# Moving a rarely taken branch, gathering every second tile in parts, and turning the biases later in a one-core attention and mixture-of-experts kernel

## The chip, the cores and the metric

The kernel runs on one core of a Trainium2 chip. The metric is the device time of one execution in microseconds (us). The time before is 1584.31 us, the median of 4 runs (1583.06 to 1585.34). A profile of one further execution was taken. Its engines are PE (TensorE matmul; PEld is its weight load), DVE (VectorE), ACT (ScalarE), POOL (GpSimd) and SP (SyncE, which issues DMAs).

## The reference, cut to what matters

The input is one image of 256 channels and 48 x 48 pixels, so 2304 tokens of width 256. All is float32.

```
x = x + Attn0(group_norm(x))            # 4 heads; softmax over all 9216 head-rows
t = tokens(x)                           # (2304, 256)
t = t + Attn1(layer_norm(t))            # soft slices: 64 slices, 8 heads
t = t + MoE(layer_norm(t))
out = t transposed back to (1, 256, 48, 48)

MoE(xf):                                # E = 8 experts, top 2 of each token
    top_w, top_i = top_k(xf @ Wg + bg, 2);  top_w = softmax(top_w)
    for e in range(8):
        h   = gelu(xf @ W1[e] + b1[e])              # 256 -> 1024
        out = out + w_dense[:, e] * (h @ W2[e] + b2[e])   # 1024 -> 256
```

## The kernel before, in words

**Start (lines 248 to 345).** The group norm needs a mean and a variance per group of 8 channels. DVE collects `bn_stats` as the image lands; PE multiplies the channel means and then `dm` (variance plus squared difference of means) with the group matrix `gm`, into the small PSUM tile `pgb`; DVE adds epsilon (`ve`, line 228), POOL raises it to the power -0.5 (`rstd`, line 229), and DVE norms the image block by block (`xn`, line 311). PE then projects q and k (lines 320 and 324) into a ring of five PSUM tiles `pp`. While PE would have nothing to do, `busy_first(n)` (line 265) gives it n matmuls whose results are not used: 14 at the very start, and 2 between the two group matmuls (line 297). They are written into the same tile `pgb` as the group sums. The 78 rows of biases (`brow`) are turned to columns (`bcol`) by a PE transposition in `spread()` (line 293), also into `pgb`. Helper classes (`InOrder`, line 52, whose issue line is L60) keep the order of `pe`, `dve`, `act` and `pool` calls as written; calls through `nc.*` are placed by a scheduler.

**Middle.** Attention 0 and the slice attention follow, and the routing: each token is given two slots, sorted by expert, in tiles of 128 slots. `slot_t` tells the token row of each slot of each tile; `used` is how many tiles are in use. Before the experts start, `busy(8, spin)` (line 1202) again gives PE eight matmuls of no use.

**Experts (lines 1343 to 1419).** There are at most 43 tiles. 36 are always there (`SURE` = 36: tiles 0 to 35), tiles 36 to 38 are "near" (`FAR` = 39), and tiles 39 to 42 are rare. For each tile s:

- `rows` gathers 128 token rows of 1 KB with one indirect DMA from POOL; `parts` instead does it with four indirect DMAs of 256 B per row (line 1237 issues all of these), so that DVE can turn the tile (`turn_parts`, line 1287) in place of PE (`turn`, line 1278: two PE transpositions into `pt` and a DVE copy to `xT`). `in_parts(s)` (line 1254) says which: before, tiles 2 to 35 except 5, 9, 13, ..., 33.
- `load_w1` has SP load 1 MB of the tile's expert (ring of two); `first` does 16 matmuls `ph` and 8 Gelus on ACT (`hid`); `second` does 8 matmuls `py`, with a function `meanwhile` called after the third of them, and DVE makes `y`; `scatter` adds `y` to the token rows in memory `t_d` by an indirect DMA from POOL.

The order is: gathers of 36, 37, 38, 0 and 1; the number `used` is loaded into every engine (line 1350); four nested branches `tc.If(used > s)` skip the rare tiles (line 1355); then tile 36, the branches for 37 and 38 (line 1386), and the loop over tiles 0 to 35 (line 1395), in which `first(s)` stands ahead of `second(s - 1)`. A tile is gathered two tiles ahead of its use. In this execution 39 tiles are in use: tiles 37 and 38 are worked on and the rare ones are jumped over.

**End (lines 1421 to 1459).** The token rows are read back after the scatter of tile 34, turned by PE, and written out. A last branch (line 1479) jumps over a second, safer version of the whole program.

Of the kernel before, what the change touches and what calls it, by code (L numbers as in the profile page):

```python
# [9 lines left out]
FP = mybir.dt.float32  # L10
# [5 lines left out]
P = 128  # L16
# [49 lines left out]
def layers(  # L66
# [181 lines left out]
    with proj, tc.tile_pool(name="ps_pj", bufs=5, space=PSUM) as ps_pj, tc.tile_pool(  # L248
# [11 lines left out]
            nc.scalar.copy(dst, pw)  # L260
            return dst

        pgb = ps_g.tile([P, 512], FP, name="pgb")

        def busy_first(n):
            for _ in range(n):
                pe.matmul(
                    pgb[:, 256:512], ones, ones.unsqueeze(1).to_broadcast([P, 2, P]), start=True, stop=True
                )

        busy_first(14)
        WqT = transposed(pj.tile([P, 2, C], FP, name="WqT"), raws["Wq"])
        pg = pgb[:, 0:4].rearrange("p (a b) -> p a b", a=2)
        pb = pgb[:, 16:94]

        st = pj.tile([P, 2, 6, 6], FP, name="st")
        mv = pj.tile([P, 2, 2], FP, name="mv")
# [12 lines left out]
        mean = pj.tile([P, 2], FP, name="mean")  # L290
        dve.tensor_copy(mean, pg[:, 0, :])

        def spread():
            pe.matmul(pg[:, 1, :], gm, dm, start=True, stop=True)
            pe.transpose(pb, brow, ident[0:78, 0:78])

        busy_first(2)
        spread()
        WkT = transposed(pj.tile([P, 2, C], FP, name="WkT"), raws["Wk"])
        rstd = pj.tile([P, 2], FP, name="rstd")  # L300
        rsqrt(rstd, pg[:, 1, :], 1e-5, 2)
        xn = t_flat[:, 0 : 2 * NT].rearrange("p (c n) -> p c n", c=2)
        dve.tensor_copy(bcol, pb)
        bq8 = pj.tile([P, 2], FP, name="bq8")
        dve.tensor_scalar(bq8, bcol[:, B_Q : B_Q + 2], 0.125, None, ALU.mult)
        WvT = transposed(pj.tile([P, 2, C], FP, name="WvT"), raws["Wv"])

        for bi, (t0, tn) in enumerate(TBLOCKS):
            toks = slice(t0, t0 + tn)
            for c in range(2):  # L310
                nc.vector.tensor_scalar(
                    xn[:, c, toks], x_sb[:, c, toks], mean[:, c : c + 1], rstd[:, c : c + 1],
                    ALU.subtract, ALU.mult,
                )
            for m in range(2):
                cols = slice(m * P, (m + 1) * P)
                pq = ps_pj.tile([P, 512], FP, name="pp", tag="pp")
                pk = ps_pj.tile([P, 512], FP, name="pp", tag="pp")
                for c in range(2):
                    nc.tensor.matmul(  # L320
                        pq[:, 0:tn], WqT[:, c, cols], xn[:, c, toks], start=(c == 0), stop=(c == 1)
                    )
                for c in range(2):
                    nc.tensor.matmul(
                        pk[:, 0:tn], WkT[:, c, cols], xn[:, c, toks], start=(c == 0), stop=(c == 1)
                    )
                for j in range(2):
                    rows = slice(j * DK, (j + 1) * DK)
                    at = (2 * m + j) * NT + t0
                    for half in range(2):  # L330
                        dst = q2[half * DK : (half + 1) * DK, at : at + tn]
                        if j == 1 and half == 1:
                            nc.scalar.activation(
                                dst, pq[rows, 0:tn], AF.Identity, bias=bq8[rows, m : m + 1], scale=0.125
                            )
                        else:
                            nc.vector.tensor_scalar(  # L337
                                dst, pq[rows, 0:tn], bcol[rows, B_Q + m : B_Q + m + 1], 0.125,
                                ALU.add, ALU.mult,
                            )  # L340
                bk_m = bcol[:, B_K + m : B_K + m + 1]
                nc.scalar.activation(kk[:, m, toks], pk[:, 0:tn], AF.Identity, bias=bk_m)
            if bi == 0:
                later_constants()
                transposed(WoT, raws["Wo"])
# [73 lines left out]
    def busy(n, bank):  # L419

        for _ in range(n):
            pe.matmul(bank[:, 0:256], ident, Wqkv_sb[:, 0, 0:256], start=True, stop=True)
# [627 lines left out]
    with gating, tc.tile_pool(name="onehot", bufs=1) as oh, tc.tile_pool(  # L1050
# [148 lines left out]
                pq[:, k, :], quad[:, k, :, :].rearrange("p q s -> p (q s)"), empties, start=True, stop=True,  # L1199
            )  # L1200
        dve.tensor_scalar(part_t, pq, 4.0, quarter, ALU.mult, ALU.add)
        busy(8, spin)

    def expert_of(s, engine):
        return nc.values_load(
# [5 lines left out]
    with tc.tile_pool(name="ps_h", bufs=1, space=PSUM) as ps_h, tc.tile_pool(  # L1211
# [5 lines left out]
        def ring(pool, n, shape, name):  # L1217
            return cycle([pool.tile(shape, FP, name=f"{name}{k}") for k in range(n)])

        ring_xs, ring_w1 = ring(fp, 2, [P, C], "xs"), ring(fp, 2, [P, 2, HID], "w1")  # L1220
        ring_xT, ring_hid = ring(fp, 3, [P, 2, P], "xT"), ring(fp, 2, [P, NHC, P], "hid")
        ring_y = ring(fp, 2, [P, C], "y")
        ring_ph, ring_py = ring(ps_h, 3, [P, 4, P], "ph"), ring(ps_y, 2, [P, C], "py")
# [2 lines left out]
        near_xs = iter([fp.tile([P, C], FP, name=f"near_xs{s}") for s in range(SURE, FAR)])  # L1226
        fin = ctx.enter_context(tc.tile_pool(name="fin", bufs=1))
        far_xs, far_w1 = fin.tile([P, C], FP, name="far_xs"), fin.tile([P, 2, HID], FP, name="far_w1")
        here = fin.tile([P, NT], FP, name="here")
        held = fin.tile([P, NTT], FP, name="held")  # L1230
        obs = cycle([fin.tile([P, 2, 512], FP, name=f"ob{k}") for k in range(3)])
# [20 lines left out]
            return xs  # L1252

        def in_parts(s):
            return 2 <= s < SURE and s % 4 != 1

        def parts(s, xs):

# [16 lines left out]
            )  # L1275
            return w1

        def turn(xs):

            pt = next(ring_pt)  # L1280
            for c in range(2):
                pe.transpose(pt[:, c, :], xs.rearrange("p (d c) -> p c d", c=2)[:, c], ident)
            xT = next(ring_xT)
            dve.tensor_copy(xT, pt)
            return xT

# [7 lines left out]
                )  # L1294
            return xT

        def first(s, xT, w1):

            e = expert_of(s, mybir.EngineType.Activation)
            hid = next(ring_hid)  # L1300
            for f0 in range(0, NHC, 4):
                ph = next(ring_ph)
                for f in range(f0, f0 + 4):
                    for c in range(2):
                        pe.matmul(
                            ph[:, f - f0, :], w1[:, c, f * P : (f + 1) * P], xT[:, c, :],
                            start=(c == 0), stop=(c == 1),
                        )
                for f in range(f0, f0 + 4):
                    act.activation(  # L1310
                        hid[:, f, :], ph[:, f - f0, :], AF.Gelu, bias=b1_e[:, bass.ds(e, 1), f],
                    )
            return hid
# [32 lines left out]
            xs[s] = rows(s, next(near_xs))  # L1346
        for s in range(2):
            w1[SURE + s] = load_w1(SURE + s, next(ring_w1))
            xs[s] = parts(s, next(ring_xs))
        used = nc.values_load(  # L1350
            used_i, min_val=0, max_val=NSL,
            skip_runtime_bounds_check_because="it is a sum of counts, cut at NSL",
        )

        with ExitStack() as more:
            for s in range(FAR, NSL):
                more.enter_context(tc.If(used > s))
                issued.clear()
                far = turn(rows(s, far_xs))
                scatter(s, second(s, first(s, far, load_w1(s, far_w1)), lambda: None))  # L1360
        issued.clear()

        def turn_next(s):
            if s in xs:
                xT[s] = (turn_parts if in_parts(s) else turn)(xs.pop(s))
# [17 lines left out]
        hid[SURE] = first(SURE, xT.pop(SURE), w1.pop(SURE))  # L1383
        w1[SURE + 2] = load_w1(SURE + 2, next(ring_w1))
        scatter(SURE, second(SURE, hid.pop(SURE), more_turns))
        with ExitStack() as more:
            for s in near[1:]:
                more.enter_context(tc.If(used > s))
                issued.clear()
                hid[s] = first(s, xT.pop(s), w1.pop(s))  # L1390
                scatter(s, second(s, hid.pop(s), lambda: turn_next(s + 1) if s + 1 in near else None))
        issued.clear()
        for s in range(2):
            w1[s] = load_w1(s, next(ring_w1))
        for s in range(SURE):
            hid[s] = first(s, xT.pop(s), w1.pop(s))
            if s + 2 < SURE:
                xs[s + 2], w1[s + 2] = parts(s + 2, next(ring_xs)), load_w1(s + 2, next(ring_w1))
            if s == 0:
                turn_next(1)  # L1400
            elif s < SURE - 2:
                scatter(s - 1, second(s - 1, hid.pop(s - 1), lambda: turn_next(s + 1)))
            if SURE - 3 <= s < SURE - 1:

                scatter(s, second(s, hid.pop(s), lambda: turn_next(s + 1) if s == SURE - 2 else None))
            if s == 4 and bad is not None:
                judge()
            if s == 6:
                dve.tensor_scalar(
                    held, lim[:, 0:NTT], -1.0, empties[:, SURE - 1 : SURE], ALU.mult, ALU.add  # L1410
                )
            if 8 <= s < 8 + len(TBLOCKS):
                t0, n = TBLOCKS[s - 8]
                shape = [P, n // P, P]
                dve.tensor_tensor(
                    here[:, t0 : t0 + n].rearrange("p (k r) -> p k r", r=P),
                    steps.unsqueeze(1).to_broadcast(shape),
                    bc(held[:, t0 // P : (t0 + n) // P], shape), ALU.is_equal,
                )
# [96 lines left out]
```

## Time and profile before

| What | Value |
|---|---|
| Median of 4 runs | 1584.31 us |
| The profiled execution's own time | 1586.42 us |
| Its span, first to last instruction | 1584.7 us |
| Mean granted clock of TensorE | 0.997 |
| PE busy | 1563.3 us (99%), 13105 matmul records |
| DVE, ACT, POOL busy | 66%, 52%, 17% |
| Experts' stage, by the timeline | 1279 us to 1558 us |
| Matmuls `ph` / `py` | 147.3 us x1248 / 142.8 us x624 |
| Gathers in parts | x104 (26 tiles), 1021 ns each on POOL |

A line of the groups reads: line, engine, operation, tiles out<-in, shapes, count | busy us, mean ns of one | idle time of the engine just before, and what ended it. A line of the waits reads: engine and tile <- what it waited for: total us, times, longest. The trace has two records for one float32 matmul, each with its weight load, and one for a PE transposition. A row whose engine ends in q is the sequencer's: it dispatches to the engine, loads registers and branches, and may be ahead of the engine. The granted clock is given by stretch of time; 0.50 means that PE ran at half speed.

### The profile page before, as it was taken

The numbers are of one execution on the slowest core, as the hardware profiler recorded it, in microseconds if no ns is written. First come the engines' busy times: TensorE is split into PE (matmuls) and PEld (weight loads), VectorE is DVE, ScalarE is ACT, GpSimd is POOL, SyncE is SP. The second block draws the span as 40 slices with busy tenths as digits, with TensorE's granted clock in tenths as the row PEclk, the third lists the DMA queues.
The fourth block names the chain that finished last, engine by engine and source line by source line (L and its number), as shares of the span: only waits on it lengthen the run. The fifth ranks groups of instructions, "written<-read, shape, count | busy, mean of one in ns | idle before, by whom it ended". The sixth has DMA issues, their size and how long they took to land. (4 is left out here: it accounts for less than half of the span.)

```text
span 1584.7 us, 32306 instructions
## 1 busy us (share of the span) xinstructions
PE 1563.3 (99%) x13105; PEld 782.0 (49%) x13105; DVE 1038.3 (66%) x1323; ACT 830.0 (52%) x1168; POOL 270.0 (17%) x210
## 2 busy tenths in 40 slices
PE   9999999999999999999999999999999999999998
PEld 5633343333333333333333333333334689999996
DVE  7578787787777778878778778787787721211111
ACT  3356565555666556656556566566554433333331
POOL 0001001011010110110101101101010135767671
PEclk9999999999999999999999999999999999999999
DMA  4000000000000000000000000000000946666765
GB/s 137 1 1 1 1 1 3 7 1 1 9 1 1 8 1 2 7 2 2 4 5 2 2 8 1 1 8 1 1 2 16 333 143 193 194 183 186 192 178 162
DMA packets 53071, 79.32 MB, mean 50 GB/s; under 512 B 22719, under 2 KB 43406, under 8 KB 47790
## 3 DMA queue, kind: packets, MB, share of 16 engines
q1 hardware_dynamic: 42834, 66.45, 13.0%
q0 software_dynamic: 9424, 10.10, 3.9%
q8 instruction: 108, 1.77, 0.4%
q10 hardware_dynamic: 652, 0.56, 0.1%
q14 instruction: 53, 0.43, 0.1%
HBM read 62.94 MB, written 12.32 MB: 47 GB/s over the span
## 5 line engine op out<-in xcount | busy, mean ns | idle before, releaser
L60 ACT ACTIVATE p<-s 128x1024 f32<-128x1024 f32 x648 | 662.7, 1023 | 471.1 <-PE s L60 470.0
L60 DVE TENSOR_TENSOR acc<-acc,p 128x1024 f32<-128x1024 f32 x612 | 749.5, 1225 | 243.3 <-ACT p L60 237.3
L60 PE MATMUL av<-p,v_sb 64*64 64x512 f32 x5184 | 676.0, 590 | 3.4 <-ACT p L60 2.2
L60 PE MATMUL s<-q,kk 64*64 64x512 f32 x5184 | 675.0, 589 | 0.5 <-DVE tn L60 0.5
L60 PEld LDWEIGHTS s<-q,kk 64*64 64x64 f32 x5184 | 202.2, 133 | 353.5 <-issue 181.5
L60 PEld LDWEIGHTS av<-p,v_sb 64*64 64x64 f32 x5184 | 195.7, 131 | 358.8 <-ACT p L60 201.4
L60 POOL PARTITION_ALL_REDUCE total<-both x17 | 71.2, 4186 | 1012.0 <-ACT p L60 833.8
L60 ACT ACTIVATE hid<-ph,bcol 128x128 f32<-128x128 f32 x312 | 89.1, 368 | 197.8 <-PE ph L60 193.7
L60 PEld LDWEIGHTS ph<-xT,w 128*128 128x128 f32 x1248 | 147.0, 194 | 2.6 <-issue 0.7
L60 PE MATMUL ph<-xT,w 128*128 128x128 f32 x1248 | 147.3, 277 | 0.6 <-issue 0.6
L60 PE MATMUL py<-w_sb,hid 128*128 x624 | 142.8, 379 | 0.0
L60 PEld LDWEIGHTS py<-w_sb,hid 128*128 128x128 f32 x624 | 115.0, 191 | 13.5
L1237 POOL DMA_INDIRECT xs<-tn_d,part_t x104 | 106.2, 1021 | 39.3 <-issue 30.5
L60 DVE TENSOR_TENSOR y<-py,b_bc 128x256 f32<-128x256 f32 x39 | 16.6, 425 | 118.0 <-PE py L60 118.0
L1237 POOL DMA_INDIRECT t_d<-y,slot_t x38 | 61.6, 1620 | 56.8 <-DVE y L60 37.7
L60 DVE STREAM_TRANSPOSE xT<-xs 128x128 f32<-128x128 f32 x52 | 13.1, 290 | 59.3 <-DMA xs<-tn_d,part_t 59.3
L60 DVE COPY xT<-pt 128x256 f32<-128x256 f32 x13 | 5.4, 424 | 53.2 <-PE pt L60 53.2
L60 DVE RECIPROCAL rinv<-rinv 128x256 f32<-128x256 f32 x17 | 29.7, 1746 | 0.0
L60 POOL TENSOR_TENSOR rstd_t<-ve,mhalf 128x2 f32<-128x2 f32 (+2 forms) x13 | 11.1, 850 | 103.6 <-DVE ve L60 95.9
L60 DVE TENSOR_TENSOR acc<-p 128x1024 f32<-128x1024 f32 x18 | 22.1, 1226 | 4.9 <-ACT p L60 3.3
L337 DVE TENSOR_SCALAR q<-pp,bcol 64x512 f32<-64x512 f32 (+1 forms) x30 | 20.8, 694 | 6.4 <-PE pp L320 6.0
L60 DVE TENSOR_REDUCE up<-av 128x512 f32<-128x1024 f32 x17 | 20.8, 1225 | 5.0 <-PE av L60 5.0
(302 smaller groups left out, 621.3 us busy)
## 6 DMA issues: line engine op xcount, KB each, us to landing
w<-in_L_ffn_W_dram SPq DMA_DIRECT2D x39, 1024.0 KB, 6.6
w_sb<-in_L_ffn_W_dram SPq DMA_DIRECT2D x8, 1024.0 KB, 10.6
t_sb<-turned SPq DMA_DIRECT2D x224, 8.0 KB, 1.8
x_sb<-in_x_dram SPq DMA_DIRECT2D x3, 576.0 KB, 3.9
xs<-tn_d,part_t POOLq DMA_INDIRECT x104
t_d<-t_sb SPq DMA_DIRECT2D x2, 768.0 KB, 11.2
tn_d<-tn SPq DMA_DIRECT2D x2, 768.0 KB, 6.3
t_sb<-t_d SPq DMA_DIRECT2D x3, 512.0 KB, 4.6
```

Source lines behind the costliest of these rows:

```text
L60: return self.tc.keep_in_program_order(getattr(self.engine, name)(*args, **kwargs))
L337: nc.vector.tensor_scalar(dst, pq[rows, 0:tn], bcol[rows, B_Q + m : B_Q + m + 1], 0.125, ALU.add, ALU.mult,)
L1237: new = nc.gpsimd.indirect_dma_start(**kwargs)
```

## The change

1. The rare tiles' branches move from before tile 36 to behind `first(0)` and `turn_next(1)`. `used` is loaded only after tile 36. The rare tiles get `xT` and `hid` tiles of their own.
2. `in_parts(s)` becomes "s even, from 2", and the ring of gathered tiles has three tiles in place of two, so that gathers are issued three tiles ahead. An even tile is turned (by DVE) after `second`; an odd one (by PE) within it.
3. `busy(8, spin)` becomes `busy(6, spin)`.
4. At the start, the filling matmuls go to a tile of the `pp` ring in place of `pgb`, 17 + 1 of them in place of 14 + 2, and the transposition of the biases moves out of `spread()` to behind the first normed half block, into a PSUM tile of its own; `bcol` and `bq8` are made there.

The diff, cut to its core:

```
-        pgb = ps_g.tile([P, 512], FP, name="pgb")
+        pgb = ps_g.tile([P, 96], FP, name="pgb")
+        spun = ps_pj.tile([P, 512], FP, name="pp", tag="pp")
         def busy_first(n):
             for _ in range(n):
                 pe.matmul(
-                    pgb[:, 256:512], ones, ...
+                    spun[:, 0:256], ones, ...
-        busy_first(14)
+        busy_first(17)
...
-        def spread():
-            pe.matmul(pg[:, 1, :], gm, dm, start=True, stop=True)
-            pe.transpose(pb, brow, ident[0:78, 0:78])
-        busy_first(2)
-        spread()
+        busy_first(1)
+        pe.matmul(pg[:, 1, :], gm, dm, start=True, stop=True)
...
-        dve.tensor_copy(bcol, pb)
-        dve.tensor_scalar(bq8, bcol[:, B_Q : B_Q + 2], 0.125, None, ALU.mult)
+        def biases():
+            pb = ps_w.tile([P, 512], FP, name="pw", tag="pw")
+            pe.transpose(pb[:, 0:78], brow, ident[0:78, 0:78])
+            nc.vector.tensor_copy(bcol, pb[:, 0:78])
+            nc.vector.tensor_scalar(bq8, bcol[:, B_Q : B_Q + 2], 0.125, None, ALU.mult)
...                                        # in the loop over blocks, after the norm
+            if bi == 0:
+                biases()
...
-        busy(8, spin)
+        busy(6, spin)
...
-        ring_xs, ring_w1 = ring(fp, 2, [P, C], "xs"), ring(fp, 2, [P, 2, HID], "w1")
+        ring_xs, ring_w1 = ring(fp, 3, [P, C], "xs"), ring(fp, 2, [P, 2, HID], "w1")
...
-            return 2 <= s < SURE and s % 4 != 1
+            return 2 <= s < SURE and s % 2 == 0
...
         for s in range(2):
             w1[SURE + s] = load_w1(SURE + s, next(ring_w1))
+        for s in range(3):
             xs[s] = parts(s, next(ring_xs))
-        used = nc.values_load(used_i, ...)
-        with ExitStack() as more:
-            for s in range(FAR, NSL):
-                more.enter_context(tc.If(used > s))
-                ...
         turn_next(SURE)
         ...
         scatter(SURE, second(SURE, hid.pop(SURE), more_turns))
+        used = nc.values_load(used_i, ...)
...
+        def rare():
+            with ExitStack() as more:
+                for s in range(FAR, NSL):
+                    more.enter_context(tc.If(used > s))
+                    issued.clear()
+                    far = turn(rows(s, far_xs), far_xT)
+                    scatter(s, second(s, first(s, far, load_w1(s, far_w1), far_hid), lambda: None))
+            issued.clear()
...
         for s in range(SURE):
             hid[s] = first(s, xT.pop(s), w1.pop(s))
-            if s + 2 < SURE:
-                xs[s + 2], w1[s + 2] = parts(s + 2, next(ring_xs)), load_w1(s + 2, next(ring_w1))
             if s == 0:
                 turn_next(1)
-            elif s < SURE - 2:
-                scatter(s - 1, second(s - 1, hid.pop(s - 1), lambda: turn_next(s + 1)))
+                rare()
+            if s + 3 < SURE:
+                xs[s + 3] = parts(s + 3, next(ring_xs))
+            if s + 2 < SURE:
+                w1[s + 2] = load_w1(s + 2, next(ring_w1))
+            if 0 < s < SURE - 2:
+                ahead = None if in_parts(s + 2) else s + 2
+                y = second(s - 1, hid.pop(s - 1), lambda: turn_next(ahead))
+                turn_next(s + 2)
+                scatter(s - 1, y)
+            elif s == 0:
+                turn_next(2)
```

## Prediction

> **What bounds the kernel now.** I read the page first: PE is busy 99% of the span and nothing else comes near. So a microsecond counts where PE idles, where its clock is lowered, or where its list of matmuls grows or shrinks. Next, PE's waits from 1200 us on:
>
> ```profile
> PE pw L60 <- ACT what L60: 3.1, 3, 1.5
> PE pt L60 <- PEq L1355: 1.6, 1, 1.6
> PE ph L60 <- issue: 0.6, 1, 0.6
> ```
>
> In the experts' stage PE waits twice, both at its start: 1.6 us for its own sequencer at line 1355 (the rare branch), and 0.6 us for the copy `xT`. It never waits for a gather, though DVE and POOL do. PE's timeline there:
>
> ```profile
> 1279.83 3.70 PE L60 MATMUL spin<-Wqkv_sb,ident 128*128 128x256 f32 x16
> 1285.11 0.48 PE L60 MATMUL pt<-ident,near_xs 128*128 128x128 f32 x2 [1.59 <-PEq L1355]
> 1286.16 5.44 PE L60 MATMUL ph<-xT,w 128*128 128x128 f32 x32 [0.56 <-issue]
> ...
> 1295.36 3.73 PE L60 MATMUL ph<-xT,w 128*128 128x128 f32 x32
> ```
>
> The same 32 records take 5.44 us the first time and 3.73 the second. The busy times by stretch (the fourth last number is POOL's, then clock, DMA share, GB/s) say why, and show the same at the program's start:
>
> ```profile
> 1286.20:1289.70 3.50, 3.50 (x17) 3.50 (x18) 0.00 (x0) 0.00 (x0) 0.00 (x0) 0.51 0.15 37
> ...
> 9.70:13.10 3.40, 2.06 (x12) 1.46 (x11) 1.92 (x8) 0.58 (x1) 0.00 (x0) 1.00 0.78 248
> 13.10:16.50 3.40, 3.40 (x14) 2.67 (x13) 1.71 (x6) 1.17 (x2) 0.73 (x1) 0.50 0.70 194
> ```
>
> After a stretch with PE idle for 2.15 us (1282.85 to 1286.27) or 1.34 us (9.70 to 13.10) the clock is halved for 3.4 us; one with 1.40 us idle (1224.80 to 1228.20) was spared. A long PE gap is paid twice: itself, and up to 3.4 x 0.5 = 1.7 us more.
>
> **1. Start of the program.** Before, the two filling matmuls write `pgb`, so they wait for DVE's `mean`, which reads it:
>
> ```profile
> 12.28 1.31 PE L60 MATMUL pgb<-ones 128*128 128x256 f32 x4 [0.70 <-DVE mean L60]
> 13.39 0.42 PE L60 MATMUL pgb<-dm,gmat 128*128 128x2 f32 x2
> 13.68 0.37 PE L60 MATMUL pgb<-ident,brow 78*128 78x78 f32 x1
> 15.70 1.08 PE L320 MATMUL pp<-t_sb,WqT 128*128 128x512 f32 x1
> ```
>
> `ve` starts at 14.09, when the transposition of the biases (same tile) ends. After: 28 filling records end at about 9.79 and six more at 0.216 bring PE to 11.09, past the landing of `Wq` (10.50); the four transpositions (0.11 apart) end at 11.53, against 11.2, so the first group sum is 0.3 later. `dm` is ready at 12.46; one filling matmul lies under that. The second group matmul runs 12.5 to 12.85 and `ve` starts at 12.9: 1.2 us sooner. POOL's 0.73 and DVE's 0.55 follow unchanged, and the first `pp` matmul starts at 14.5 in place of 15.70. PE's idle time in the stretch is now some 0.3 us, so the clock stays up: 0.8 us at half speed (15.70 to 16.51) costs nothing more, 0.4 saved. The bias transposition now stands among projections, 0.1 on PE. DVE's order puts `bcol` after four norms (4 x 0.48 from 13.9, so 16.1), before the first q tile is full (16.4); five `pp` tiles at 1.72 us each cover the rest. From there on PE is the bound, so this arrives at the end. Sum **-1.5 us**; bounds -0.7 (clock still falls, a late copy) and -1.7.
>
> **2. Start of the experts.** Twelve spin records end at 1282.5, not 1283.4. Without the branch ahead of it, `turn(36)` waits for its gather: issued 1279.09, and by the landing records 15 of its 16 signals are in by 1282.20, the last at 1284.32. That straggler comes after two instruction fetches (1282.04 and 1282.31), which I put down to the branches that are now gone. So `pt` at 1282.5 in place of 1285.11: -2.6. PE then idles only the 0.56 for the copy, so the clock should hold: 5.44 becomes 3.73, -1.7. Sum **-4.3 us**; bounds: -0.7 if the last signal stays at 1284.32 (2.3 us idle, clock falls), -4.4 at most. Loading `used` and the two branches of line 1386 lie under PE's own queue: these branches took 0.07 to 0.2 us and PE had no gap.
>
> **3. The branch in its new place.** This is the step that decides.
>
> ```profile
> L1355 PEldq COMPARE_BRANCH  x1: 4318/4318/4318, 1280.3 to 1280.3; - x1
> L1479 PEldq COMPARE_BRANCH  x1: 4057/4057/4057, 1578.1 to 1578.1; - x1
> ```
>
> Both far jumps hold PE's sequencer for 4.1 to 4.3 us; 0.46 more (two semaphores, a wait) passed until PE's next record (1284.65 to 1285.11). The first hid because 3.2 us of spin were queued behind it. Behind `first(0)` and `turn(1)`, how much is queued? The register load of line 1205 stands at that very place before the change: it starts at 1311.44 and the next `py` runs at 1313.44. In every tile that lead is 1.99 us, 18 records; the sequencer is then stopped by a full queue. So PE idles 4.2 + 0.46 - 1.99 = 2.7 us. More than 1.4 us of that falls into one clock stretch, so the clock falls: +1.7. The jump skips the same four bodies, too far for what is at hand in both places. Sum **+4.4 us**. Bounds: 0 if the target happens to be at hand (near jumps took 0.2 us), +6 if the fetch queues behind W1's megabyte. The other engines jump too: ACT needs some 2 us between two sets of Gelus and has 5; DVE 0.6; SP 0.9 while it waits for `first(0)` anyway; POOL waits for its outstanding transfers (line 1355 has it wait until 1288) and sends the last two parts of tile 4 after that, over 10 us before their use. `scatter(0)` behind it waits for `y` longer still.
>
> Here the trace and the Trainium skill part. "TensorE: Matmul & The Clock Gate", in its introductory table, gives the queue as 64 deep: that would be 32 records or 3.57 us, a stall near 1.1 us and no clock loss, and the whole sum would become -2.6 us; the row of line 1205 shows 18 records, and I go by it. The same page, section "Why this matters for your kernels", calls only gaps over some 3 us harmful: by that the clock would hold after a 2.7 us gap and the sum be -1.0; the 1.34 us row above speaks against it.
>
> **4. Gathers.** PE turned 13 tiles, now 22 (0, 1, 36 to 38, and 3 to 35 odd). A turn within the stream costs 0.23:
>
> ```profile
> 1395.04 1.30 PE py L60 x6
> 1396.34 0.23 PE pt L60 x2
> 1396.57 2.16 PE py L60 x10
> ```
>
> 9 x 0.23 = **+2.1 us**, all on PE; bounds 1.9 and 2.3. POOL saves 9 x 3 gathers of 1.02 us, and DVE 18 transpositions for 9 copies: worth nothing, as PE waits for neither. Gathering three ahead hides what PE never waited for; it gives even tiles 14 us more or less to land in.
>
> **Sum:** -1.5 - 4.3 + 4.4 + 2.1 = **+0.7 us**. Against the profiled execution's 1586.42 (span 1584.7 and 1.7 around it) that is 1587.1; the median of the runs lies 2.1 below the profiled one, and I carry the difference over: 1584.31 + 0.7 = **1585.0 us**.
>
> **Rivals.**
> - *The jump is hidden* (0.13): the target is at hand or the queue is deeper there. Step 3 is 0: 0.7 - 4.4 = -3.7, 1580.6 us, faster. For it: the near jumps. Against: both far jumps cost over 4 us whatever was queued.
> - *The clock holds after the jump* (0.12): -1.7, 1583.3 us, no change. For it: the spared stretch with 1.40 us idle.
> - *The first gather lands late* (0.15): PE starts tile 36 at 1284.5 whether or not the branch is ahead of it, and loses its clock as before. Step 2 is -0.7: 4.3 us, 1588.6 us, slower. It decides from a landing of about 1283.9 on, when the idle time passes 1.4 us. For it: the straggler of 1284.32. A fetch queued behind W1 (step 3, +6) comes to the same side.
> - *The parts scheme relieves POOL and that pays*: PE has no wait for POOL in the stage, so its price is 0; it is within the forecast.
>
> **How the numbers follow.** A measurement of this kernel tells about 0.2% (3.2 us) from no change. The forecast (0.60) and the clock's case (0.12) are within that, together 0.72; faster 0.13; slower 0.15. The range takes in the bounds of steps 2 and 3: 1580.6 to 1588.6.
>
> **What would show it.** Right: first `pp` matmul near 14.5 at full clock; `pt` of tile 36 at 1281 (1282.5 less 1.5), `ph` 3.7 us long; a PE gap of 2.7 us after `first(0)`, ended by PE's sequencer at the new branch, and half clock after it; 44 `pt` records. Wrong: no gap at the branch (faster), or a gap before tile 36 ended by the gather (slower).

## The result, and the profile after

The changed kernel takes 1587.27 us (median of 31 runs, 1584.47 to 1589.90), the kernel before 1584.38 us (51 runs). The ratio is 1.0016, with a 95% interval of 1.0011 to 1.0021: 2.5 us more (1.7 to 3.3). That is less than the 0.2% that the prediction takes as no change, and inside its range; the forecast was 0.7 us more. The profiled execution took 1589.90 us, with a span of 1587.6. Of the 2.5 us some 0.5 lie outside the span: time less span is 1.75 us on average in 33 executions of the kernel before (second group below) and 2.29 in 33 of the changed one.

PE's waits from 1200 us on, the lines that answer to those of before:

```profile
PE ph L60 <- PEq L1391: 1.9, 1, 1.9
...
PE pt L60 <- issue: 1.2, 1, 1.2
PE ph L60 <- DMA t_sb<-t_d: 1.2, 1, 1.2
...
PE ph L60 <- DVE xT L60: 0.5, 1, 0.5
```

The 1.6 us at the branch ahead of tile 36 are gone. In their place stand 1.9 us at the branch's new line, 1391, and 1.2 us before one turn, `pt`, which was not foreseen. The wait for `t_sb`, when the token rows are read back at the end, is 1.2 us in place of 0.5. PE's timeline shows where they are:

```profile
14.83 1.13 PE L322 MATMUL pp<-t_sb,WqT 128*128 128x512 f32 x2 [0.72 <-DVE t_sb L311]
...
1281.70 0.39 PE L60 MATMUL pt<-ident,near_xs 128*128 128x128 f32 x2
1282.61 3.84 PE L60 MATMUL ph<-xT,w 128*128 128x128 f32 x32 [0.52 <-DVE xT L60]
...
1308.06 0.40 PE L60 MATMUL pt<-ident,xs 128*128 128x128 f32 x2
1310.34 5.44 PE L60 MATMUL ph<-xT,w 128*128 128x128 f32 x32 [1.88 <-PEq L1391]
...
1337.15 4.91 PE L60 MATMUL py<-w_sb,hid 128*128 x22
1343.27 0.47 PE L60 MATMUL pt<-ident,xs 128*128 128x128 f32 x2 [1.20 <-issue]
```

The `ph` of tile 36 runs at full clock (3.84 us in place of 5.44). That of tile 1, behind the branch, is now the long one. The busy times by stretch (the clock is the third last number) say that its clock fell:

```profile
1306.60:1310.10 3.50, 1.86 (x17) 1.67 (x15) 0.83 (x3) 2.22 (x8) 1.84 (x2) 1.00 0.59 80
1310.10:1313.50 3.40, 3.16 (x16) 3.19 (x17) 0.00 (x0) 0.00 (x0) 1.04 (x1) 0.59 0.79 299
```

The jump itself, in the rows of line 1391:

```profile
L1391 PEldq COMPARE_BRANCH  x1: 3577/3577/3577, 1306.3 to 1306.3; - x1
```

In this execution the clock fell once more, which the prediction did not have: in the slice attention, behind the wait of 1.40 us whose stretch was spared in the profile before. The stretches as they lie here:

```profile
1225.40:1228.81 3.41, 1.79 (x14) 1.60 (x15) 1.88 (x8) 1.59 (x7) 0.00 (x0) 1.00 1.03 356
1228.81:1232.22 3.41, 3.41 (x12) 3.00 (x13) 1.77 (x7) 0.34 (x1) 0.00 (x0) 0.50 1.10 354
```

PE had been 1.5 us ahead of the first profile before (1216.52 against 1218.02 at the matmul `pb`), and at 1232.2 the two are level. The second profile of the changed kernel, below, has nothing of this.

### The profile page after: what moved, and what is told of

Its sections match the earlier page's. It is cut to its first block, busy times and chain, and to the rows that moved or that the text cites. A ratio compares the mean times of both kernels' runs of the same rounds, so it can differ in the third digit from the quotient of the medians.

```text
span 1587.6 us, 32252 instructions
## 1 busy us (share of the span) xinstructions
PE 1565.7 (99%) x13123; PEld 784.3 (49%) x13123; DVE 1035.6 (65%) x1314; ACT 829.9 (52%) x1168; POOL 242.4 (15%) x183
## 3 DMA queue, kind: packets, MB, share of 16 engines
q8 instruction: 108, 1.77, 0.5%
## 5 line engine op out<-in xcount | busy, mean ns | idle before, releaser
L1241 POOL DMA_INDIRECT xs<-tn_d,part_t x68 | 69.5, 1022 | 27.1 <-issue 19.8
L60 DVE COPY xT<-pt 128x256 f32<-128x256 f32 x22 | 9.2, 423 | 79.6 <-PE pt L60 79.6
L1241 POOL DMA_INDIRECT xs<-tn_d,slot_t x19 | 20.0, 1051 | 5.8 <-issue 5.5
```

The source lines that it names most:

```text
L60: return self.tc.keep_in_program_order(getattr(self.engine, name)(*args, **kwargs))
L1241: new = nc.gpsimd.indirect_dma_start(**kwargs)
```

## The experiments

The kernels ran in three groups of four, each group on one chip beside the kernel before (an expectation says "call" for group). In the second group the kernel before took 1584.7 us (33 runs). In the first and the third it took 1602.2 and 1602.6 us, with what is shown at the end of this section, so a time of those groups is compared only with times of the same group.

**The change taken apart (second group).**

The changed kernel again:

> The changed kernel itself, to stand beside the other three on their chip, and to tell two readings of the four runs before apart, in which the kernel before took 1602 us and only kernels with 17 tiles in parts took 1585 to 1588. If that was the chip of those runs and nothing else, and this is another chip: before 1584, this 2.5 us over it. If the kernel before is near 1600 here too: this 1586 to 1588, some 14 under it. In the profile: the jump on PE 3.4 to 3.8 us with a gap of 1.7 to 2.1 us behind first(0); the wait before the turn of tile 7 (1.2 us) comes back only if that gather lands as late again (6.4 us after its issue).

1587.59 us, ratio 1.0019 (1.0010 to 1.0028): as recorded. Jump 3.59 us, gap 1.90, half clock behind it, and again a wait before tile 7's turn:

```profile
1341.39 0.48 PE L60 MATMUL pt<-ident,xs 128*128 128x128 f32 x2 [1.00 <-issue]
```

Only the start changed (item 4 of the change, nothing else):

> The kernel before with only the changed start (fillings into the pp ring, 17 + 1 of them, the biases turned behind the first normed block). The prediction had -1.5 with a first projection at 14.5; the trace of the changed kernel has it at 14.83 and Attention 0 1.14 us sooner. Theory 1: 1.1 under before. Rival (the saving is lost again in the routing, where PE waits for DVE and ACT and the clock's stretches fall otherwise): within 0.3 of before.

1582.56 us, ratio 0.9988 (0.9979 to 0.9997): 1.9 us less (0.5 to 3.3), the only clear gain among the runs of one part. Its first projection starts at 14.26:

```profile
12.22 0.38 PE L60 MATMUL pgb<-dm,gmat 128*128 128x2 f32 x2 [0.16 <-DVE mean L60]
...
14.26 1.12 PE L322 MATMUL pp<-t_sb,WqT 128*128 128x512 f32 x2 [0.65 <-DVE t_sb L311]
```

Only the branch moved, with its own tiles and 6 fillings:

```
 # kernel before
-        busy(8, spin)
+        busy(6, spin)
-        (used = ...; the four nested branches, ahead of turn_next(SURE))
...
+                rare()          # behind turn_next(1), in the loop's s == 0
```

> The kernel before with only the branch moved behind first(0) and turn(1) (own tiles for the rare bodies, used loaded behind tile 36, 6 filling matmuls in place of 8); the start and the gathers as before. Theory 1: -4.3 at tile 36 (no wait for the jump, full clock) and +3.7 at the new place (1.9 idle, 1.7 half clock, 0.1 around it): 0.6 under before, and down to 2.3 under it in executions in which the gap is cut by the clock's stretches and the clock holds. Rival (the first gather is late without the branch too): tile 36 starts 2 us after its filling ends, and the time is 2 to 4 us over before.

1584.98 us, ratio 1.0000 (0.9991 to 1.0009). Tile 36 gains as in the changed kernel, and the new place takes it all back. The jump is longer here, 4.38 us, and so is the gap (the row of line 1388, then the waits):

```profile
L1388 PEldq COMPARE_BRANCH  x1: 4379/4379/4379, 1305.2 to 1305.2; - x1
```

```profile
PE ph L60 <- PEq L1388: 2.7, 1, 2.7
```

A gap of 2.7 us and 1.7 us of half clock are the 4.4 of the prediction's step 3. The two parts sum to -1.9 and the whole is +3.0 (1.0019), so what is left, the gathers, costs some 4.9, known to no better than 2 us either way. The profiles explain 3.3 of it: nine turns (2.1) and the wait before tile 7's (1.2). Another 0.5 is the time outside the span, which is 1.75 and 1.77 us in the runs of the branch and of the start alone, as before.

**What the jump costs, and when it hides (first group).** One rare tile less:

```
-                for s in range(FAR, NSL):
+                for s in range(FAR, NSL - 1):
```

> The changed kernel with three rare tiles in place of four: tile 42, which this execution does not use, is left out, so the branch behind first(0) jumps over a body of about 114 PE instructions less (343 in place of 457). Theory 1 (the four steps of the prediction, with a wait for the gather of tile 7 added): the changed kernel is 2.5 us slower than before because the jump costs 1.9 us of PE idle time and 1.7 us of half clock. If the 3.58 us of the compare-and-branch are the loading of code that is not at hand, the nearer target falls inside what is at hand: the branch takes under 0.5 us on PE, no gap, no half clock, and the time is 1.2 us under before. Rival A (any taken branch over the rare tiles costs 3 to 4 us on PE): gap and clock stay, 2.5 us over before.

1585.37 us, with the kernel before at 1602.18 (0.9899, 0.9873 to 0.9924). The jump fell to less than half, not to under 0.5:

```profile
L1391 PEldq COMPARE_BRANCH  x1: 1645/1645/1645, 1306.5 to 1306.5; - x1
```

```profile
1308.26 0.40 PE L60 MATMUL pt<-ident,xs 128*128 128x128 f32 x2
1309.77 3.84 PE L60 MATMUL ph<-xT,w 128*128 128x128 f32 x32 [1.11 <-DVE xT L60]
```

PE's gap is 1.1 us, now ended by DVE's `xT`, which the jump no longer covers, and the clock held. The same group's kernel with `judge()` later, which keeps the full jump, took 1587.67: 2.3 more. So not every taken branch over the rare tiles costs 3 to 4 us; Rival A is out. The profiles also record transfers of instructions. In each of the 27 jumps of PE that took 3.35 us or more (the branch and the last branch of the program, in 14 profiles), one of 16 KB on queue q8 starts 0.9 to 2.0 us after the jump does (here in the changed kernel, the queue's row for 1306.3 to 1309.87):

```profile
q8 instruction: 1, 0.02, 1.9%
```

In the jump of 1.65 us there is none. That fits a fetch of code that is not at hand, and it is no matter of distance alone: the last branch, over a whole second program, takes 4.06 us in the kernel before. Why 1.65 and not 0.2 stays open.

The branch behind `second(0)`:

```
-                rare()                      # behind turn_next(1), s == 0
...
                 y = second(s - 1, hid.pop(s - 1), lambda: turn_next(ahead))
+                if s == 1:
+                    rare()
```

> The changed kernel with the rare tiles' branches behind second(0) in place of first(0): the records queued ahead of the branch are then py (one per 0.216 us) in place of ph (one per 0.112 us). Theory 1 with a queue counted in records (18): the lead is some 3.7 us in place of 2.0, the jump of 3.6 us and 0.44 of semaphores leave a gap of 0.3 us, and the clock holds: 1.0 us under before. Rival C (the sequencer's lead is a time of 2 us whatever is queued): the gap of 1.9 us and the half clock stay, 2.5 over before.

1585.67 us (0.9905, 0.9879 to 0.9932), 2.0 under the `judge()` kernel of its group. The jump is as long as ever, but it starts 3.4 us ahead of the end of PE's queue (1312.9 to 1316.35), not 2.2 (1306.3 to 1308.46 in the changed kernel):

```profile
1314.03 2.32 PE L60 MATMUL py<-w_sb,hid 128*128 x10
1317.22 3.81 PE L60 MATMUL ph<-xT,w 128*128 128x128 f32 x32 [0.87 <-DVE y L60]
```

```profile
L1391 PEldq COMPARE_BRANCH  x1: 3817/3817/3817, 1312.9 to 1312.9; - x1
```

Counted in records that PE had still to run, the lead is the same: 16 `ph` and 2 `pt` in the changed kernel, 4 `ph`, 12 `py` and 2 `pt` here, 18 in both. It is a count, not a time: Rival C is out.

**The wait before tile 7's turn.** The profile names no releaser ("issue"); the order of PE's instructions and the landing of the gather point to it. The scheduler puts half of `second(4)`, with that turn in it, ahead of `judge()` and of tile 5's `ph`. The gather, issued at 1336.83, is then needed 5 us later, and its last landing record is at 1343.18 (6.35 us), 0.09 ahead of the turn. The W1 load of tile 6 was issued 0.5 us behind it. In the second profile it is the same: 0.5 us, and a landing after 6.1. In the two kernels just shown the load follows 1.5 us behind the gather, the gather lands in 2.9 us, and the same turn, in the same place, waits for nothing. With `judge()` one tile later:

```
-            if s == 4 and bad is not None:
+            if s == 5 and bad is not None:
```

> The changed kernel with judge() called after first(5) in place of first(4), so that the turn of tile 7 no longer stands ahead of tile 5's ph on PE. Theory 1: the wait before that turn (1.2 us idle, 1.45 in all) goes, 44 turns remain: 1.0 us over before. Rival (the gather of a whole tile beside a W1 load is late wherever it stands): a wait of about the same length at this or another turn, 2.5 over before.

> The changed kernel with judge() behind first(5), once more, since the times of the kernel before beside its first run were 18 us off. In two profiles of the changed kernel PE waits 1.2 and 1.0 us before the turn of tile 7, whose gather landed 6.3 us after its issue, beside a W1 load issued 0.5 us behind it. Theory 1: with the turn behind tile 5's ph the wait is gone: 1.2 us under the changed kernel (1587.3 to 1587.6), so 1.3 to 1.7 over before. Rival (a wait of one profile, or it moves to another turn): 2.5 to 2.9 over before, as the changed kernel.

1587.67 and 1587.89 us (0.9915 and 0.9911 to a kernel before of 1602). In the timeline of the second of them the turn stands behind tile 5's `ph` (1339.07), and nothing waits:

```profile
1335.61 3.62 PE L60 MATMUL py<-w_sb,hid 128*128 x16
1339.07 3.73 PE L60 MATMUL ph<-xT,w 128*128 128x128 f32 x32
1342.64 1.46 PE L60 MATMUL py<-w_sb,hid 128*128 x6
1343.93 0.39 PE L60 MATMUL pt<-ident,xs 128*128 128x128 f32 x2
```

But there the W1 load too is issued 1.5 us behind the gather, which lands in 2.9 us, so these runs don't tell the order from the landing; and no run moved the load alone. What the change is worth in time stays open, since both runs fell into groups in which PE lost 1.8 us at tile 36, which the changed kernel's two profiles don't show.

**Both mended together (second group):** the branch behind `second(0)` and `judge()` later.

> The changed kernel with the branch behind second(0) and judge() behind first(5). Theory 1: of the 3.7 us at the branch a gap of 0.9 us without half clock is left, so 2.8 under the changed kernel, and up to 1.4 more in executions in which the gather of tile 7 would have been late: 0.3 to 1.7 under before. Rival (the loss is in the gathers and turns alone, 22 turns): no better than the changed kernel.

1584.26 us, ratio 0.9994 (0.9985 to 1.0003): 3.3 under the changed kernel beside it, level with before. The gap at the branch is 0.58, with the clock at full speed to PE's last matmul:

```profile
1315.26 3.81 PE L60 MATMUL ph<-xT,w 128*128 128x128 f32 x32 [0.58 <-DVE y L60]
```

**The rule of before for the gathers in parts (first and third group),** alone and with both mends:

```
-            return 2 <= s < SURE and s % 2 == 0
+            return 2 <= s < SURE and s % 4 != 1
```

> The changed kernel with the rule of before for gathers in parts (all but 5, 9, ..., 33), still three tiles ahead. Theory 1: 9 turns of 0.23 us leave PE (-2.1), and with tile 7 in parts PE's wait of 1.2 us before its turn (1.45 with what lies around it) goes too: 1.0 us under before. If only the turns count and some other turn waits in its place: 0.4 over before. Rival B (the gathers in parts are free either way and the loss is all at the branch): 2.5 over before, unchanged.

> The changed kernel with the rule of before for gathers in parts, once more for the same reason. Theory 1: 9 turns of 0.23 (2.1) and the wait before tile 7's turn (1.2) go: 3.3 under the changed kernel, so 0.4 to 0.8 under before. Rival B (the gathers are free, the loss is at the branch): as the changed kernel, 2.5 to 2.9 over before. Rival D (26 tiles in parts three tiles ahead starve some other transfer, as in the first call, where this kernel took 1598 us): over 1590.

> All that the runs so far speak for, together: the changed start, the branch behind second(0), judge() behind first(5), and the gathers in parts by the rule of before. Theory 1: 2.1 under the kernel with the late branch and 17 tiles in parts (1584.3), so 1582.2, 2.3 under before and level with the changed start alone (1582.6). If the gains at tile 36 (4.3 in the profiles) are worth as much in the median: 1579.5, 5 under before. Rival D as above: over 1590.

1597.94, 1597.30 and 1592.91 us beside a kernel before of 1602 (0.9981, 0.9959 to 1.0002; 0.9966, 0.9947 to 0.9986; 0.9955, 0.9933 to 0.9977). So the price of the turns could not be weighed in time, and the best version could not be named: of the runs in the second group it is the changed start alone.

**The kernel before again (third group).**

> The kernel before itself, for a second profile of it: the prediction took its clock losses from one execution, with three stretches of half clock (behind the start, at tile 36, at the end; mean clock 0.997, where 33 other executions had 3.2 us lost on the mean against 4.75 here). Theory 1: the wait at tile 36 (1.6 and 0.6 us) and at the start (0.7 and 0.5) are there again, but not both stretches of half clock in each execution: clock 0.998 and about 1.6 us less time. Rival (the half clocks belong to the kernel and come each time): the same three stretches, and 1586.

1600.76 us (0.9986, 0.9956 to 1.0016): neither time of the expectation, but its profile answers two questions. First, the start, in its timeline and its busy times by stretch: half clock does not come each time at the start (at tile 36 it does, in all three profiles of kernels with the branch ahead of it).

```profile
10.49 0.63 PE L60 MATMUL pw<-ident,Wq_raw 128*128 128x128 f32 x4 [1.41 <-DMA Wq_raw<-in_L_conv_Wq_dram]
...
15.27 1.98 PE L320 MATMUL pp<-t_sb,WqT 128*128 128x512 f32 x4 [0.78 <-DVE t_sb L311]
```

```profile
13.10:16.50 3.40, 2.62 (x16) 1.80 (x15) 2.14 (x7) 1.07 (x2) 0.73 (x1) 1.00 0.76 203
```

The same program with the same waits kept full clock and reached 1219 us 1.75 us sooner than in the first profile. Second, where the 16 us go (an example from the timeline):

```profile
1443.03 1.55 PE L60 MATMUL py<-w_sb,hid 128*128 x6
1445.46 0.59 PE L60 MATMUL py<-w_sb,hid 128*128 x2 [0.88 <-issue]
1446.20 1.89 PE L60 MATMUL py<-w_sb,hid 128*128 x8 [0.15 <-issue]
1447.93 1.15 PE L60 MATMUL ph<-xT,w 128*128 128x128 f32 x6
1449.90 0.72 PE L60 MATMUL ph<-xT,w 128*128 128x128 f32 x5 [0.82 <-issue]
1451.33 4.13 PE L60 MATMUL ph<-xT,w 128*128 128x128 f32 x21 [0.71 <-issue]
```

PE's weight loads go on in groups, some 0.72 us apart, and no semaphore holds them ("issue"). I read this as instructions that arrive late; no run tested it. All four profiles of kernels with 26 tiles in parts of those two groups have it in the stream of tiles; the four with 17 tiles in parts have none there, and neither has any profile of the second group or of the first comparison, with 26 or 17. Why it comes in some groups and not in others stays open; the record gives chip 2 for the first and the second group and 15 for the third, so the chip's number does not tell them apart. The changed kernel itself did not run in those groups.

## Why the prediction was right, point by point

- **Bound by PE:** right within the span; each microsecond found there is one in which PE idles, runs at half clock or has more to do. The 0.5 us outside the span are not PE's.
- **Step 1, the start (-1.5):** the mechanism right, the size within its bounds. In time the part is worth 1.9 alone (0.5 to 3.3). In the profiles it is some 1.1: PE's turn of `W_sb`, at the start of Attention 0, begins at 48.41, 47.60 and 47.80 in the three with the old start, at 47.27 and 46.68 in the changed kernel's two and at 46.70 with the start alone. The half clock that step 1 saves came in the first of the three old ones only. The first `pp` at 14.83 and not 14.5: the fillings end at 11.37, not 11.09, since full clock was granted only from 6.84 us on. In the run of the start alone it came at 4.60, and they end at 10.49.
- **Step 2, tile 36 (-4.3):** right. From the last filling's start to the end of `ph` the changed kernel gains 4.35. The gather was there at 1281.70, so the rival of a late gather fell.
- **Step 3, the branch (+4.4):** the mechanism was right in each link (jump, 18 records of lead, gap, half clock), the size a little high: 1.88 + 1.71 and 0.16 around them, 3.75, since this jump took 3.58 and not 4.2. In the run of the branch alone gap and half clock are 2.68 + 1.71, the 4.4. On both points set against "TensorE: Matmul & The Clock Gate" of the Trainium skill the row held. Its introductory table's queue of 64, taken as 32 records, would by an estimate have left a gap of some 0.5 us; it was 1.88. Its section "Why this matters for your kernels" fears only gaps over some 3 us; 1.88 and 1.90 lowered the clock in the two profiles.
- **Step 4, the turns (+2.1):** 22 turns, 9 x 0.23 = 2.07, as forecast. "Gathering three ahead hides what PE never waited for" was wrong at one place: the wait of 1.2 us at tile 7's turn (1.0 in the second profile). I had counted turns, not asked when each is due.
- **The sum (+0.7, measured +2.5):** the wait adds 1.2, the shorter jump takes 0.6, and the time outside the span adds 0.5, which the prediction took as unchanged ("1.7 around it"): 0.7 + 1.2 - 0.6 + 0.5 = 1.8, within the interval (1.7 to 3.3). The last 0.7 is not assigned; the longer wait for `t_sb` at the end (1.2 and 0.8 us in place of 0.5) and a start worth less than 1.5 are candidates. The clock is not the cause as far as the record goes. By the mean clocks the kernel before loses 3.2 us (33 executions), the changed one 2.2 (33) and 3.0 (11 more): 0.1 to 1.0 less, where the steps counted on 0.4 less. (The mean clock also counts half clock behind PE's last matmul, where it costs nothing.) Carrying over the 2.1 between profiled run and median did no harm either: in the changed kernel it is 2.6.
- **The clock's rival** is no matter of the kernel alone: at least 5 of the 33 executions of the changed kernel with a clock on record, those with 1.000, held it behind the same jump. The prediction's "More than 1.4 us of that falls into one clock stretch, so the clock falls" is no rule; the last section has what the traces show. The two `judge()` runs held the clock too:

```profile
1310.35 3.81 PE L60 MATMUL ph<-xT,w 128*128 128x128 f32 x32 [1.68 <-DVEq L1391]
...
1310.43 3.81 PE L60 MATMUL ph<-xT,w 128*128 128x128 f32 x32 [2.14 <-PEq L1391]
```

- **Luck:** 2.5 us lies midway between the forecast (0.7) and the rival of a late gather (4.3), and the range of 8 us would have held with a step gone wrong. What speaks for the prediction is the profile, in which its steps stand one by one.

## What to carry to other kernels

A jump over code that is rarely run took about as long wherever it stood (3.35 to 4.38 us over the four bodies); put it where the most time is queued, behind the longest matmuls, since the queue counts records. Before trusting a gather that is "three ahead", find in the engine's own order when its user is due and which big load is issued beside it. And before crediting a removed wait with the half clock behind it, see in more than one profile whether the clock really falls: it did in one of three at the start, in three of three at tile 36.

## What the hardware showed that was not expected

- Half clock came in stretches of 3.41 us, which in every profile begin a whole number of 3.41 us after the first grant of full clock (in the changed kernel's first profile at 1228.81 and 1310.73, 24 of them apart). So a gap's second price depends in part on how it lies against them: 2.14 us, split into 0.6 and 1.55 by such a border, kept the clock; 1.88 and 1.90, whole within one stretch, lost it. PE's idle time in a stretch does not settle it either: 1.68 us (the first `judge()` run) kept the clock, 1.62 (the slice attention) and 1.34 (the start before) lost it.
- The far jump took PE 3.35 to 4.38 us over four bodies and 1.65 over three; ACT, DVE and POOL took 0.06 to 0.07 for the same branch.
- A gather of 128 rows of 1 KB landed in 2.9 us where 1 MB of W1 was issued 1.5 us behind it (four profiles), and in 6.1 and 6.35 us where it was issued 0.5 us behind (two). No run moved the load alone.
